# A new order around the first scores, in the short units and in the last units of a cross-attention and expert kernel

## The chip, the cores and the metric

One core of a Trainium2 chip runs the whole program. The metric is the device time of one execution in microseconds (us), as the median of several runs. PE is the matrix engine (TensorE), ACT is ScalarE, DVE is VectorE, POOL is GpSimd, and SP is the engine whose queue issues most of the DMAs.

## The reference

`x` is 32 x 100 x 512 and the context 32 x 722 x 512, all in float32. With 16 heads of 32:

```python
x = x + xattn(layernorm(x), ctx, ctx, WQ, WK, WV, Wfc, bfc)
x = x + ffn(layernorm(x), gate_w, Wg, Wu, Wd, Ws_g, Ws_u, Ws_d)

def xattn(Q, K, V, ...):
    q, k, v = heads(Q @ WQ.T), heads(K @ WK.T), heads(V @ WV.T)
    scores = q @ k.T / sqrt(32)
    scores = where(tril(ones(Sq, Skv)), scores, -inf)
    return softmax(scores) @ v ... @ Wfc.T + bfc

def ffn(h, ...):
    probs = softmax(h @ gate_w.T).transpose(0, 2, 1)       # 16 experts
    w, idx = top_k(probs, 12)                              # 12 tokens per expert and batch row
    out = scatter_add(((gelu(xt @ Wg.T) * (xt @ Wu.T)) @ Wd.T) * w)
    return out + (gelu(h @ Ws_g.T) * (h @ Ws_u.T)) @ Ws_d.T   # one shared expert
```

The mask is causal and a row of `x` has 100 positions, so only the first 100 positions of the context count, and the kernel takes only those: 3200 tokens on both sides.

## The kernel before

Products that feed the result are computed from a high and a low half of each operand in three matmuls (`mm3`): the high half is a cast to a shorter matmul format on ACT, the low half is the rest, formed by a subtraction on DVE or POOL. In the text "split" is this pair of steps.

**Stages.** The prologue loads and splits the weights of K, V and Q and computes keys and values of context blocks 0 and 1 (256 tokens each). Then come 32 attention units, `u = 0` to `31`. Unit `u` stands for a superblock of four batch rows (`sb = u // 4`, 400 tokens) and a group of four heads (`c = u % 4`, 128 columns). Units 0 to 28 run in one loop, and units 29 to 31 (`NU - 3` to `NU - 1`) and what is left behind them are written out one after the other in `last_units`. Behind the attention follow the shared expert and the 16 experts (`F.run`), which the diff does not touch.

**What one unit of the loop does**, in the order of the code:
- SP issues the loads: `kload(u)` (keys back from DRAM, `kt`), `ctx_load`, `x_load` and `xt_load` (rows and columns of x).
- `scores(u - 1)`: 16 small matmuls into the one set of score banks (`sc`), from `q` and `kt`.
- `y_keep(u - 3)` splits the output of `values` (ACT, then DVE) and so frees its bank.
- `sm_max(u - 1, 0 / 1)`: eight masked maxima each on DVE; `sm_sub`: the subtraction on POOL.
- `xt_split` splits 128 columns of x of the next superblock; `qproj(u)`, and `qkeep(u)` copies the result to `q` on ACT.
- `sm_exp(u - 1, 0 / 1)` on ACT, `sm_sum` (sum and reciprocal) on DVE, `sm_mul` on POOL.
- `p_turn(u - 2, 0..3)` transposes the probabilities on PE into the two `ms` banks, and `p_keep` copies them to `pt` on ACT.
- `kproj` and `vproj` compute a chunk of keys and a block of values of a coming context block; `kkeep` and `vkeep` copy them out of their bank on ACT and write them to DRAM (`kD`, `vD`). There are two banks `kv`, shared with `qproj`.
- `ctx_split(jn, d)`: cast on ACT, low half on POOL. `x_stats` (DVE) and `x_rstd` (POOL) give the scale of each row, which `sm_exp` applies; the mean is taken out of the weights of Q instead, by `wq_sum` (DVE), `wq_mean` (PE) and `wq_keep` (DVE, then a split).
- `values(u - 2)` multiplies the copies `pt` with `v` (loaded by `vload`, 800 KB for four units).

A context block from 2 on has three groups of 128 tokens but four chunks of keys, so in every fourth unit (u = 4, 8, ..., 28) there is a `kproj` and no `vproj`. These are the short units: their `values` come right behind the last two transposes.

**The order.** PE, ACT, DVE, SP and, in the attention, POOL run their instructions in the order in which the code issues them. An instruction that waits holds up all that stands behind it on its engine, and a DMA waits in SP's queue in the same way. Tiles come from rings of a fixed number of buffers (two `ms` and two `kv` banks, one `sc`, two `kt`, three `xr`, four `cr`, five `p`), and a new tile waits for the last reader of the buffer that it takes.

**The last units.** `pr` prepares the first 384 tokens of the expert part while units 29 to 31 run: `load_x`, `bias` (POOL), `fc` (PE), `add` (DVE), `stats` (DVE), `rsqrt` (POOL), `norm` (DVE), `store` (a write to DRAM), `turn` (transposes on PE, cast on ACT, low half on DVE), each for the tiles 0, 1, 2 of 128 tokens. `F.preps[1]` does the same for the next 256 tokens. `F.chunk_load`, `chunk_cast` (ACT) and `chunk_low` (POOL) bring and split the first expert weights, and `F.begin` starts the first `gu` matmuls.

Lines of the profile: L56 all `mm3` matmuls, L104 and L105 the cast and the low half of `split`, L138 and L139 the same of `ctx_split`, L223 `kkeep`, L229 `kload`, L234 `vload`, L249 `qkeep`, L259 `scores`, L270 `sm_max`, L279 `sm_sub`, L285 `sm_exp`, L290 and L291 `sm_sum`, L296 `sm_mul`, L302 `p_turn`, L307 `p_keep`, L317 `values`, L1059 `bias`, L1068 `add`, L1082 `rsqrt`, L1089 `norm`, L1000 and L1001 `turn`.

Of the kernel before, what the change touches and what calls it, by code (L numbers as in the profile page):

```python
# [7 lines left out]
F32 = mybir.dt.float32  # L8
# [52 lines left out]
def attention(tc, K, F):  # L61
    nc = tc.nc
    with ExitStack() as ctx, ExitStack() as kvctx:
# [153 lines left out]
        def kkeep(j, c, pk):  # L217
            t0, n = KSTART[j] * 128, KVB[j] * 128
            if j < 2 and c > 1:
                kk = qp.tile([128, SB], F32, name="q")  # L220
            else:
                kk = kkp.tile([128, KMAX], F32, name="kk")
            nc.scalar.copy(kk[:, 0:n], pk[:, 0:n])  # L223
            nc.sync.dma_start(K.kD[:, c, t0:t0 + n], kk[:, 0:n])
# [107 lines left out]
        def prologue():  # L332
# [48 lines left out]
            for c in range(NC4):  # L381
                kkeep(1, c, kproj(1, c))
                if c == 0:
                    wq_sum(0, wq[0])
                    wq_sum(1, wq[1])
                    kload(0)
                    for b in range(4):
                        x_load(0, b)
                else:
                    ctx_split(2, c - 1)  # L390
                if c == 1:
                    wq_mean(0)
                    wq_keep(0, wq[0])
                    xt_split(0, 2)
                if c == 2:
                    xt_split(0, 3)
                    wq_mean(1)
                    wq_keep(1, wq[1])
                if c > 1:
                    wq_sum(c, wq[c])  # L400
            xt_load(1, 0)
            ctx_load(3, 0)
            vkeep(1, 0, vproj(1, 0))
            return wq
# [16 lines left out]
        def last_units(pr):  # L421

            gp, mt = nc.gpsimd, pr.pt

            def maxes(u):
                for hb in range(2):
                    sm_max(u, hb)
                    sm_sub(u, hb)
# [3 lines left out]
            kload(u)  # L432
            for i in range(pr.nt):
                pr.load_x(i)
            y_keep(u - 3)
            kload(u + 1)
            vload(nsb - 1)
# [19 lines left out]
            pr.bias(0)  # L457
            maxes(u - 1)
            pr.bias(1)
# [3 lines left out]
            turns(u - 2, 0, 1)  # L463
            sm_exp(u - 1, 0)
            keeps(u - 2, 0, 1)
            sm_exp(u - 1, 1)
            pr.fc(1)
            for hb in range(2):
                sm_sum(u - 1, hb)
                sm_mul(u - 1, hb)  # L470
            turns(u - 2, 2, 3)
            keeps(u - 2, 2, 3)
            pr.norm(0)
            pr.add(1)
            kload(u + 1)
            F.chunk_load()
            values(u - 2)
# [4 lines left out]
            pr.store(0)  # L482
            pr.bias(2)
            pr.stats(1)
            pr.rsqrt(1)
            maxes(u - 1)
            pr.norm(1)
            qkeep(u, qproj(u))
# [4 lines left out]
            keeps(u - 2, 0, 1)  # L493
            sm_exp(u - 1, 0)
            sm_exp(u - 1, 1)
            pr.fc(2)
            sm_sum(u - 1, 0)
            sm_mul(u - 1, 0)
            pr.store(1)
            turns(u - 2, 2, 3)  # L500
            keeps(u - 2, 2, 3)
            sm_sum(u - 1, 1)
            sm_mul(u - 1, 1)
            pr.pt = lambda: ps_kv.tile([128, D], F32, name="kv").rearrange("p (c t) -> p c t", c=NC4)
# [3 lines left out]
            pr.add(2)  # L508
            pr.turn(1)
            pr.stats(2)  # L510
            F.chunk_cast(0, 0)
            pr.rsqrt(2)
# [11 lines left out]
            pr.norm(2)  # L524
# [11 lines left out]
            pr.store(2)  # L536
# [22 lines left out]
        with tc.manual_schedule(engines={mybir.EngineType.Pool}):  # L559
            wq = prologue()  # L560
            for u in range(NU - 3):
# [40 lines left out]
                if u == 0:  # L602
                    for b in range(3):
                        x_stats(0, b)
                    wq_mean(2)
# [10 lines left out]
                x_stats(*xn)  # L616
                if xn[1] == 3:
                    x_rstd(xn[0])
                if a is not None:
                    sm_exp(a, 1)  # L620
                    sm_sum(a, 0)
                    sm_mul(a, 0)
# [3 lines left out]
                if c == 1:  # L626
                    vload(sb)
                if back is not None:
# [3 lines left out]
                    p_keep(back, 3)  # L632
                if kv and not vv:
                    kkeep(j, ck, pk)
                if a is not None:
                    sm_sum(a, 1)
                    sm_mul(a, 1)
                if jn in blocks:
                    ctx_split(jn, d)
                if u in FC_AT:  # L640
                    F.fc_split(FC_AT.index(u), fr)
                if u == 0:
                    wq_keep(2, wq[2], nc.gpsimd)
                    vkeep(1, 1, vproj(1, 1))
                if vv:
                    vkeep(j, ck, vproj(j, ck))
                if back is not None:
                    values(back)
# [713 lines left out]
```

## Time and profile before

| what | value |
|---|---|
| median of 3 runs | 1670.34 us (1667.94 to 1670.6) |
| the profiled execution | 1668.51 us |
| its span, from the first to the last instruction | 1666.7 us, mean granted PE clock 0.999 |
| PE busy (matmuls) | 1641.7 us, 98% |
| DVE, ACT, POOL busy | 916.7, 695.9, 627.6 us |
| attention (prologue and units) | to about 371 us of the span |
| one full unit, one short unit | about 10.4 us, about 8.6 us |

Times in the text count from the start of the span. In a line of the timeline the columns are: start, duration, engine, line, operation, output and inputs with their shapes, and in brackets how long the engine had stood idle just before and what released it. In a line of the waits: who waited for whom, the total in us, how many times, the longest. In a line of the windows: the stretch and its length, then for each engine the busy us and the number of instructions, then the granted PE clock, the share of the DMA engines and the GB/s.

### The profile page before, as it was taken

To read this page: it belongs to the slowest core of one execution; us is meant where nothing else is said; L and a number is where in the kernel's file an instruction comes from. 1 tells how busy PE (TensorE), PEld (TensorE's weight loads), DVE (VectorE), ACT (ScalarE), POOL (GpSimd) and SP (SyncE) were. 2 spreads that over 40 slices of the span, in tenths; PEclk is the share of its full clock that TensorE was granted. 3 is DMA by queue.
4 is the path that set the end of the run, shared out by engine and by line. 5 is a ranking of instruction groups with operands and counts; after the bars stand their busy time and mean duration, and the time that the engine had idled before them with its cause. 6 is when DMAs were issued, how large, how long until landed. Compare 5 with 4: busy or idle time off the path is not lost.

```text
span 1666.7 us, 27942 instructions
## 1 busy us (share of the span) xinstructions
PE 1641.7 (98%) x10722; PEld 1503.5 (90%) x10722; DVE 916.7 (55%) x2175; ACT 695.9 (42%) x1152; POOL 627.6 (38%) x502
## 2 busy tenths in 40 slices
PE   8999999999999999999999999999999999999999
PEld 7788888879989998999999999999999999999998
DVE  5778777665433434343665555555555555555542
ACT  4666666553111111112444444444444444444442
POOL 1878777680110011010653344443344343344001
PEclk9999999999999999999999999999999999999999
DMA  7566655565312223211455555455555455555452
GB/s 236 167 188 204 196 176 169 194 192 187 114 62 84 76 90 126 82 46 41 155 172 161 161 167 154 153 150 161 163 160 161 153 149 163 163 155 163 138 160 61
DMA packets 113637, 244.02 MB, mean 146 GB/s; under 512 B 16625, under 2 KB 64978, under 8 KB 113504
## 3 DMA queue, kind: packets, MB, share of 16 engines
q1 hardware_dynamic: 100000, 216.54, 39.7%
q0 software_dynamic: 13088, 25.22, 7.9%
q8 instruction: 84, 1.38, 0.3%
q10 hardware_dynamic: 416, 0.48, 0.1%
q14 instruction: 49, 0.40, 0.1%
HBM read 188.46 MB, written 53.73 MB: 145 GB/s over the span
## 4 chain that ended last, share of the span: by engine, by line
PE 91%; DVE 2%; ACT 2%; POOL 2%; DMA 1%; issue 1%; SPq 0%; ACTq 0%; POOLq 0%; DVEq 0%
PE gu L56 49%; PE dn L56 24%; PE kv L56 9%; PE m L56 3%; PE ms L302 2%; PE ms L317 2%; POOL p L279 1%; PE sc L259 1%; DVE p L270 1%; ACT p L285 1%; ACT pt L307 1%; DMA xr<-xT 1%; DVE y L105 0%; DMA raw<-wA 0%; PE m L1143 0%
## 5 line engine op out<-in xcount | busy, mean ns | idle before, releaser
L56 PE MATMUL gu<-xh,whl 128*128 128x384 f32 (+1 forms) x3200 | 641.3, 332 | 0.0
L56 PEld LDWEIGHTS gu<-xh,whl 128*128 128x128 f32 x3200 | 555.8, 188 | 20.3 <-issue 1.3
L967 POOL DMA_INDIRECT gx<-xnD,iq x192 | 245.4, 1278 | 395.4 <-DVE big L1010 296.3
L56 PE MATMUL dn<-whl,hh 128*128 128x512 f32 x1168 | 366.3, 395 | 0.0
L770 DVE TENSOR_TENSOR whl<-wraw,whl 128x1536 fp32r<-128x1536 f32 x142 | 249.7, 1759 | 197.7 <-ACT whl L769 197.7
L56 PE MATMUL gu<-xl,whl 128*128 128x384 f32 (+1 forms) x1600 | 335.8, 331 | 0.0
L56 PEld LDWEIGHTS gu<-xl,whl 128*128 128x128 f32 x1600 | 279.1, 188 | 0.0
L804 ACT CAST hh<-g 128x384 fp32r<-128x384 f32 (+1 forms) x200 | 101.0, 505 | 407.6 <-DVE g L801 407.6
L56 PEld LDWEIGHTS dn<-whl,hh 128*128 128x128 f32 x1168 | 215.7, 188 | 35.7
L801 DVE TENSOR_TENSOR g<-g,gu 128x384 f32<-128x384 f32 (+1 forms) x200 | 108.2, 541 | 253.6 <-PE gu L56 247.3
L769 ACT CAST whl<-wraw 128x1536 fp32r<-128x1536 f32 x142 | 209.8, 1477 | 56.1 <-PE dn L56 53.1
L56 PE MATMUL dn<-whl,hl 128*128 128x512 f32 x584 | 230.5, 395 | 0.0
L800 ACT ACTIVATE g<-gu 128x384 f32<-128x384 f32 (+1 forms) x200 | 96.2, 481 | 232.6 <-PE gu L56 232.5
L805 DVE TENSOR_TENSOR hl<-g,hh 128x384 fp32r<-128x384 f32 (+1 forms) x200 | 111.6, 558 | 114.2 <-ACT hh L804 114.2
L1022 POOL DMA_INDIRECT out_dram<-x,isl x48 | 77.7, 1619 | 171.0 <-ACT x L1021 161.3
L56 PEld LDWEIGHTS dn<-whl,hl 128*128 128x128 f32 x584 | 109.6, 188 | 26.0
L279 POOL TENSOR_TENSOR p<-p,mx 100x800 f32<-100x800 f32 x64 | 105.7, 1672 | 43.0 <-DVE mx L270 42.4
L296 POOL TENSOR_TENSOR p<-p,sm 100x800 f32<-100x800 f32 x64 | 97.2, 1524 | 29.1 <-DVE sm L291 27.8
L270 DVE CUSTOM_DVE_ANT_0 p<-sc,mask 100x100 f32<-100x100 f32 x512 | 95.3, 256 | 0.0
L1059 POOL TENSOR_TENSOR x<-x,bfc 128x512 f32<-128x512 f32 x23 | 30.6, 1354 | 154.7 <-DMA x<-x 154.7
L285 ACT ACTIVATE p<-p,rstd 100x400 f32<-100x400 f32 x128 | 73.7, 624 | 20.3 <-POOL p L279 20.3
L1011 ACT CAST xh<-big 128x512 fp32r<-128x512 f32 x59 | 36.6, 621 | 101.1 <-DVE big L1010 101.1
(158 smaller groups left out, 1579.3 us busy)
## 6 DMA issues: line engine op xcount, KB each, us to landing
wraw<-wE SPq DMA_DIRECT2D x144, 768.0 KB
yD<-y SPq DMA_DIRECT2D x31, 400.0 KB
xr<-xT SPq DMA_DIRECT2D x32, 200.0 KB
vD<-vt SPq DMA_DIRECT2D x25, 256.0 KB
kt<-kD SPq DMA_DIRECT2D x32, 200.0 KB
v<-vD SPq DMA_DIRECT2D x8, 800.0 KB
xnD<-xn SPq DMA_DIRECT2D x25, 256.0 KB
out_dram<-x SPq DMA_DIRECT2D x25, 256.0 KB
```

Of the source, the lines that this page charges most:

```text
L56: r = nc.tensor.matmul(out, t[0][a], t[1][b], start=(first and i == 0), stop=(last and i == n - 1))
L270: nc.vector.tensor_tensor_reduce(out=p[:, bb, h, :], in0=sc[:, h, cs], in1=mask, scale=ISCALE, scalar=NEG, op0=ALU.add, op1=ALU.max, accum ...
L279: nc.gpsimd.tensor_tensor(pv, pv, mx[:, :, None].to_broadcast([S, 8, S]), ALU.subtract)
L285: nc.scalar.activation(p[:, bb], p[:, bb], AF.Exp, scale=rstd[:, b:b + 1])
L296: nc.gpsimd.tensor_tensor(pv, pv, sm[:, :, None].to_broadcast([S, 8, S]), ALU.mult)
L769: nc.scalar.copy(h, r)
L770: nc.vector.tensor_tensor(l, r, f32(h), ALU.subtract)
L800: nc.scalar.activation(g[:, 0:t], pg[:, 0:t], AF.Gelu)
L801: nc.vector.tensor_tensor(g[:, 0:t], g[:, 0:t], pu[:, 0:t], ALU.mult)
L804: nc.scalar.copy(hh[:, 0:t], g[:, 0:t])
L805: nc.vector.tensor_tensor(hl[:, 0:t], g[:, 0:t], f32(hh[:, 0:t]), ALU.subtract)
L967: nc.gpsimd.indirect_dma_start(out=g[:, k, :], out_offset=None, in_=self.K.xn.rearrange("t (a f) -> (t a) f", f=128), in_offset=bass.Indir ...
```

## The change

The diff touches only the order of the attention, and one copy is new.
- **First keys.** `kkeep` copies the first 400 tokens of key chunk 0 from the banks straight into `kt` on DVE, in two pieces (256 and 144 columns), and `kload(0)` goes.
- **Centring and splits.** `ctx_split(2, 0..2)` move to the end of the prologue. `wq_keep(2)` and `wq_keep(3)` move from units 0 and 1 to the middle and end of unit 1, behind exponentials of the first softmax; `xt_split(1, 0)` moves from unit 0 to the end of unit 1 and `xt_split(1, 1)` to unit 2, where `xt_split(1, 2)` is as well. Unit 1 has an order of its own. `x_load` and `x_stats` run one unit further ahead.
- **Short units.** They have no `ctx_split`; the unit before does two. The two context loads that belong to them are likewise issued together. In six of them (u = 4 to 24) `scores(u)` stand ahead of `values(u - 2)`, where the flag `ahead` tells the next unit to leave its own scores out and to put `y_keep` behind the first maxima.
- **Last units.** `vload` of the last superblock comes ahead of the x rows, and `bias`, `fc`, `add`, `stats`, `rsqrt`, `norm`, `store`, `qproj` and the transposes of units 30 and 31 stand in a new order.

```diff
@@ kkeep
             nc.scalar.copy(kk[:, 0:n], pk[:, 0:n])
+            if c == 0 and j < 2:
+                if j == 0:
+                    cur["k", 0] = ktp.tile([128, SB], F32, name="kt")
+                m = min(n, SB - t0)
+                nc.vector.tensor_copy(cur["k", 0][:, t0:t0 + m], pk[:, 0:m])
             nc.sync.dma_start(K.kD[:, c, t0:t0 + n], kk[:, 0:n])
@@ prologue
                     wq_sum(0, wq[0])
                     wq_sum(1, wq[1])
-                    kload(0)
                     for b in range(4):
                         x_load(0, b)
-                else:
-                    ctx_split(2, c - 1)
+                if c == 3:
+                    ctx_split(2, 0)
...
             xt_load(1, 0)
+            x_load(1, 0)
             ctx_load(3, 0)
             vkeep(1, 0, vproj(1, 0))
+            ctx_split(2, 1)
+            ctx_split(2, 2)
@@ last_units
             u = NU - 3
             scores(u - 1)
             kload(u)
+            vload(nsb - 1)
             for i in range(pr.nt):
                 pr.load_x(i)
             y_keep(u - 3)
             kload(u + 1)
-            vload(nsb - 1)
...
             pr.bias(0)
+            pr.bias(1)
             maxes(u - 1)
-            pr.bias(1)
             pr.stats(0)
             pr.rsqrt(0)
             qkeep(u, qproj(u))
             turns(u - 2, 0, 1)
+            keeps(u - 2, 0, 1)
             sm_exp(u - 1, 0)
-            keeps(u - 2, 0, 1)
             sm_exp(u - 1, 1)
             pr.fc(1)
+            pr.norm(0)
             for hb in range(2):
                 sm_sum(u - 1, hb)
                 sm_mul(u - 1, hb)
             turns(u - 2, 2, 3)
             keeps(u - 2, 2, 3)
-            pr.norm(0)
             pr.add(1)
             kload(u + 1)
             F.chunk_load()
+            pr.store(0)
+            pr.bias(2)
             values(u - 2)
 
             u = NU - 1
             scores(u - 1)
             y_keep(u - 3)
-            pr.store(0)
-            pr.bias(2)
+            maxes(u - 1)
+            pr.fc(2)
+            pr.add(2)
             pr.stats(1)
             pr.rsqrt(1)
-            maxes(u - 1)
             pr.norm(1)
-            qkeep(u, qproj(u))
+            pr.stats(2)
+            pr.rsqrt(2)
             F.ask(1, lambda: ps_kv.tile([128, D], F32, name="kv"))
             F.preps[1].load_x(0)
             F.preps[1].load_x(1)
             turns(u - 2, 0, 1)
             keeps(u - 2, 0, 1)
+            qkeep(u, qproj(u))
+            turns(u - 2, 2, 3)
+            keeps(u - 2, 2, 3)
             sm_exp(u - 1, 0)
             sm_exp(u - 1, 1)
-            pr.fc(2)
-            sm_sum(u - 1, 0)
-            sm_mul(u - 1, 0)
+            pr.norm(2)
             pr.store(1)
-            turns(u - 2, 2, 3)
-            keeps(u - 2, 2, 3)
-            sm_sum(u - 1, 1)
-            sm_mul(u - 1, 1)
+            pr.store(2)
+            for hb in range(2):
+                sm_sum(u - 1, hb)
+                sm_mul(u - 1, hb)
...
             pr.turn(0)
             pr.pt = mt
             values(u - 2)
-            pr.add(2)
             pr.turn(1)
-            pr.stats(2)
             F.chunk_cast(0, 0)
-            pr.rsqrt(2)
...
-            pr.norm(2)
...
-            pr.store(2)
@@ the loop over units 0 to 28
-                xn = divmod(u + 3, NC4)
+                xn = divmod(u + 4, NC4) if u + 4 < NU else None
+                nov = kv and not vv
...
-                if jl in blocks and (jl, dl) != (3, 0):
-                    ctx_load(jl, dl)
-                if u + 4 < NU:
-                    x_load(*divmod(u + 4, NC4))
+                for dd in {3: (), 2: (2, 3)}.get(dl, (dl,)):
+                    if jl in blocks and (jl, dd) != (3, 0):
+                        ctx_load(jl, dd)
+                if u + 5 < NU:
+                    x_load(*divmod(u + 5, NC4))
...
-                if a is not None:
+                if a is not None and not ahead:
                     scores(a)
-                if u - 3 >= 0:
+                if u - 3 >= 0 and not ahead:
                     y_keep(u - 3)
                 if a is not None:
                     sm_max(a, 0)
                     sm_sub(a, 0)
+                    if ahead:
+                        y_keep(u - 3)
                     sm_max(a, 1)
                     sm_sub(a, 1)
-                if xs:
+                if u == 2:
+                    xt_split(1, 1)
+                if xs and u > 1:
                     xt_split(sb + 1, c)
                 qkeep(u, qproj(u))
+                if u == 1:
+                    vload(0)
...
                 if u == 1:
-                    wq_keep(3, wq[3])
-                if a is not None:
+                    sm_exp(a, 0)
+                    wq_keep(2, wq[2])
+                    sm_sum(a, 0)
+                    sm_mul(a, 0)
+                if a is not None and u > 2:
                     sm_exp(a, 0)
...
+                if u == 2:
+                    sm_exp(a, 0)
...
+                if u == 1:
+                    sm_exp(a, 1)
+                    sm_sum(a, 1)
+                    sm_mul(a, 1)
...
+                if u == 1:
+                    vkeep(j, ck, vproj(j, ck))
+                    wq_keep(3, wq[3])
+                    xt_split(1, 0)
...
-                if jn in blocks:
-                    ctx_split(jn, d)
+                for dd in {3: (), 2: (2, 3)}.get(d, (d,)) if u else (3,):
+                    if jn in blocks:
+                        ctx_split(jn, dd)
...
-                    wq_keep(2, wq[2], nc.gpsimd)
                     vkeep(1, 1, vproj(1, 1))
-                if vv:
+                if vv and u > 1:
                     vkeep(j, ck, vproj(j, ck))
+                ahead = nov and u < NU - 4
+                if ahead:
+                    scores(u)
                 if back is not None:
                     values(back)
```

More of the change, by code (lines that the diff above doesn't have):

```diff
@@ L423, in last_units, with kt_bank @@
             gp, mt = nc.gpsimd, pr.pt
+            def kt_bank():
+                return ps_kv.tile([128, D], F32, name="kv").rearrange("p (c t) -> p c t", c=NC4)
             def maxes(u):
@@ L493, in last_units @@
             keeps(u - 2, 0, 1)
+            qkeep(u, qproj(u))
+            turns(u - 2, 2, 3)
+            keeps(u - 2, 2, 3)
             sm_exp(u - 1, 0)
             sm_exp(u - 1, 1)
-            pr.fc(2)
-            sm_sum(u - 1, 0)
-            sm_mul(u - 1, 0)
+            pr.norm(2)
             pr.store(1)
-            turns(u - 2, 2, 3)
-            keeps(u - 2, 2, 3)
-            sm_sum(u - 1, 1)
-            sm_mul(u - 1, 1)
-            pr.pt = lambda: ps_kv.tile([128, D], F32, name="kv").rearrange("p (c t) -> p c t", c=NC4)
+            pr.store(2)
+            for hb in range(2):
+                sm_sum(u - 1, hb)
+                sm_mul(u - 1, hb)
+            pr.pt = kt_bank
             pr.turn(0)
@@ L560, in attention @@
             wq = prologue()
+            ahead = False
             for u in range(NU - 3):
@@ L596, in attention @@
                     sm_sub(a, 0)
+                    if ahead:
+                        y_keep(u - 3)
                     sm_max(a, 1)
                     sm_sub(a, 1)
-                if xs:
+                if u == 2:
+                    xt_split(1, 1)
+                if xs and u > 1:
                     xt_split(sb + 1, c)
                 qkeep(u, qproj(u))
+                if u == 1:
+                    vload(0)
                 if u == 0:
-                    for b in range(3):
+                    for b in range(4):
                         x_stats(0, b)
+                    x_rstd(0)
                     wq_mean(2)
@@ L615, in attention @@
                     p_keep(back, 1)
[L616 to L619, printed above, removed]
+                if u == 2:
+                    sm_exp(a, 0)
+                if xn:
+                    x_stats(*xn)
+                    if xn[1] == 3:
+                        x_rstd(xn[0])
+                if a is not None and u > 1:
                     sm_exp(a, 1)
@@ L625, in attention @@
                     kkeep(j, ck, pk)
-                if c == 1:
+                if u == 1:
+                    sm_exp(a, 1)
+                    sm_sum(a, 1)
+                    sm_mul(a, 1)
+                if c == 1 and u > 1:
                     vload(sb)
@@ L632, in attention @@
                     p_keep(back, 3)
+                if u == 1:
+                    vkeep(j, ck, vproj(j, ck))
+                    wq_keep(3, wq[3])
+                    xt_split(1, 0)
                 if kv and not vv:
                     kkeep(j, ck, pk)
-                if a is not None:
+                if a is not None and u > 1:
                     sm_sum(a, 1)
                     sm_mul(a, 1)
-                if jn in blocks:
-                    ctx_split(jn, d)
+                for dd in {3: (), 2: (2, 3)}.get(d, (d,)) if u else (3,):
+                    if jn in blocks:
+                        ctx_split(jn, dd)
                 if u in FC_AT:
```

## The prediction

> **What bounds the kernel now.** The page first: the matmuls of TensorE (PE) fill 98% of the span, so only PE's idle time and its slow stretches can be won.
>
> ```profile
> span 1666.7 us, 27942 instructions
> ...
> PE 1641.7 (98%) x10722; PEld 1503.5 (90%) x10722; DVE 916.7 (55%) x2175; ACT 695.9 (42%) x1152; POOL 627.6 (38%) x502
> ...
> PEclk9999999999999999999999999999999999999999
> ```
>
> Idle are 25.0 us. Next PE's timeline, where a bracket ends a line in which PE stood still and names its releaser. Everything that the diff touches runs before 376 us; from 400 to 700 us PE is busy 100%, so behind the attention nothing changes and any time won there reaches the end. From 25 to 371 us the brackets add to 18.4 us:
>
> ```profile
> 38.09 0.96 PE L259 MATMUL sc<-kt,q 32*100 32x100 f32 x32 [2.81 <-ACT q L249]
> ...
> 39.88 1.53 PE L56 MATMUL kv<-xnl,wh 128*128 128x400 f32 x4
> ...
> 50.55 0.99 PE L56 MATMUL kv<-xnh,wh 128*128 128x400 f32 x4 [1.33 <-ACT kk L223]
> ...
> 57.31 0.86 PE L302 MATMUL ms<-ident,p 100*100 100x100 f32 x8 [1.50 <-ACT pt L307]
> ```
>
> ```profile
> 200.05 0.89 PE L317 MATMUL ms<-pt,v 100*32 100x100 f32 x32 [0.86 <-ACT pt L307]
> 208.02 0.94 PE L302 MATMUL ms<-ident,p 100*100 100x100 f32 x8 [0.98 <-ACT pt L307]
> 241.20 0.89 PE L317 MATMUL ms<-pt,v 100*32 100x100 f32 x32 [0.86 <-ACT pt L307]
> ```
>
> The 0.86 comes seven times, 40 us apart (79.88 to 321.26): `values` of each short unit waits for ScalarE's copies of the probabilities. The last units hold 1.77, 1.27 and three small ones. Third, the clock behind the 2.81 (the second last number but one is PEclk):
>
> ```profile
> 40.00:41.00 1.00, 1.00 (x5) 0.99 (x4) 0.96 (x3) 0.00 (x0) 0.00 (x0) 0.50 0.00 0
> ```
>
> Last, the timeline of all engines and SP's waits for what holds those releasers:
>
> ```profile
> 37.12 0.53 ACT L104 CAST xnh<-xr 128x400 fp32r<-128x400 f32 x1 [6.75 <-DMA xr<-xT]
> ```
>
> ```profile
> SPq L229 <- DMA kD<-kk: 4.3, 1, 4.3
> ```
>
> ScalarE sat 6.75 us before a split of x whose DMA went out late, because SP stood 4.3 us on the key load; `qkeep(0)`, and so the first scores, were queued behind.
>
> **A: up to unit 3.** I lay the new order out with the durations of before (times are its clock). The two new DVE copies have no row: between 0.20 (128x48 copy from PSUM) and 0.56 (128x400 from PSUM, two inputs); I take 0.3 and 0.25. The first falls into DVE's 1.29 us idle before 11.35. The second waits for `kproj(1, 0)` (about 20.5); the two `wq_sum` behind it on DVE (1.03 each) start at 20.9, not 18.83, and `wq_mean(0)` holds PE 0.15. Should the copy have to stand behind ScalarE's (0.37) of the same bank, A loses 0.4 at most. [...]
>
> ScalarE no longer waits 1.54 for `cr` at 24.00, so the bank copies that held PE 0.47 and 0.71 come in time: that of `kkeep(1, 2)` ends at 25.2 (ScalarE then has one cast of wq and one of x before it, no more), that of `kkeep(1, 3)`, behind the second centring on DVE (26.3 to 27.0) and its cast, at 28.0. So `vproj(1, 0)` starts at 25.4 and `qproj(0)` at 28.35 (was 29.52). `qkeep(0)` follows it, and scores(0) follow `vproj(1, 1)` (2.93) at 34.0 instead of 38.09: the 2.81 is gone. Then the clock: it read 0.50 for 3.9 us behind that gap and twelve matmuls took 3.76 instead of 2.2; minus 1.55. [...] Unit 1: scores 0.89, `qproj` 2.24, `kproj` 2.24, `vproj` 2.93: scores(1) at 42.3 (was 48.26).
>
> Given back in unit 2: DVE carries in unit 1 sixteen maxima (2.94), two centrings (0.67 each) and low halves (0.69), two sums with reciprocals (1.2 each), `x_stats` (0.87), a split (0.6): it starts the next maxima at 46.8, 4 us late, since it must wait for POOL and ScalarE between. POOL's subtractions end at 49.9 and 51.6 (1.67 each behind a first maximum at 48.2), the second exponential at 52.8 (1.15), `kkeep(2, 1)` at 53.25, and copies 2 and 3 of the probabilities, queued behind it on ScalarE, at 54.1: `values(0)` starts at 53.75, 1.65 after `vproj`, and its transposes wait 0.4. Two splits of x there (0.6 to 1.8 each, 1.80 being a row beside POOL's subtraction) can add 0.5, unit 3 waits 0.7 to 1.1. scores(3) come at 65.75 to 66.6 against 72.10: A = minus 5.8, bounds 4 and 7. Moved DMAs: without `kload(0)` the four x rows go out at 23.7 instead of 28.7 and land by 30.3 at the 300 GB/s of that stretch, when `x_stats` needs them; `vload(0)` stands on SP for the last write of `vD`, ahead of the key write of unit 1, which nobody reads for three units; `xt_load(1, 3)` stands there until 46.8, needed at 56.
>
> **B: short units.** Six of seven (not u = 28) put 0.83 of scores between the transposes and `values`; ScalarE's copies need 0.86 from the last transposes on; should they be late by more (the exponential before them waits on POOL), the excess shows again as a wait of `values`. The inputs of scores are ready: the score banks were read 3 us earlier. The next unit's maxima then start at 242.1 instead of 243.3 (behind a sum that ends 242.08), and POOL, without the low half of context (1.0) and the rstd pair (1.27) there, starts subtracting 1.1 us earlier: the chain moves ahead as much as PE. Two context splits in the unit before fit: ScalarE had 0.81 idle before `vt`, POOL 1.95 before its subtraction, against 0.54 and 1.0 (unit 11, with a split of Wfc as well, may lose 0.2). `y_keep` of the next unit moves behind the first maxima: its bank is wanted by the second transposes at 244.4, and DVE is through with it at 244.1. `rstd` goes to the unit before, where POOL has room; the doubled context loads on SP meet free tiles, since their splits now come a unit earlier. The 0.98 at 208 (the split of the gate's weights, 1.45 on DVE ahead of the maxima) stays. B = 6 x 0.83 = minus 5.0; bounds minus 5.2 and minus 1 (wait back in the next unit).
>
> **C: last units.** v is issued 3.2 us earlier, so the 1.77 goes, but not all is won: ScalarE's copies ended only at 339.47. New on POOL: bias(1) (1.30) stands ahead of both subtractions; they end at 338.2 instead of 337.1, both exponentials now precede copies 2 and 3, `values(28)` starts at 339.95 (was 340.61). On DVE norm(0) now stands before the sums and waits for POOL's rsqrt until 339.25; the products end at 344.15 (were 342.2), bias(2) at 345.45, subtractions at 348.45, rsqrt(1) 349.4. Scores(31) start at 350.85 (were 352.27): minus 1.4. But DVE still owes norm(1), stats(2), a wait for rsqrt(2), norm(2) (352.7), two sums (2.4), two low halves (1.4) and y(29) (0.55): 357.05, before 354.98. The next transposes need y(29)'s bank: PE, done with `fc(0)` at 354.6, waits 2.45. Then transposes and keeps, `fc(1)` 358.75 to 361.65, and the exponentials push the last xh to 363.6: the expert part starts at 363.65, before 362.20. C = plus 1.4; bounds minus 2 and plus 3.5, as two POOL waits more or less decide.
>
> **Sum.** 5.8 + 5.0 - 1.4 = 9.4. The profiled execution took 1668.5 (span 1666.7), so 1659.1; the median of before is 1.8 above that execution and its runs spread 2.7, so I say 1660. Faster or slower by 0.2% (3.3 us) is about what can be told from no change.
>
> **Rivals.**
> - *C also wins.* If the norms find POOL free (0.58 against the 2.61 that norm(0) took beside POOL's products), DVE is through near 355: C = minus 2, 1657. Against: I count three waits there. 0.17.
> - *The clock halves again.* 2.45 us idle at 354.6 is close to the 2.81 that halved it for 3.9 us; 1.77 did not. Price 1.9: 1662. 0.12. [...]
> - *B moves its wait.* Transposes 3 of the following unit already start the moment their bank is copied (x8 took 0.95, not 0.86, at 248.06). If the chain does not come earlier, B keeps 1: 1664. 0.09.
> - *Slower.* x rows 0 and 1 (256 KB each) now queue behind v (800 KB), whose wait in before ended 13.3 us after its issue. At that pace v lands at 337.3, x0 at 341.6, x1 at 345.9. In unit 30 add(0) stands first on DVE, with y(27), the maxima and all else behind it; on POOL bias(1) stands ahead of both subtractions. bias(1) then ends at 347.2, the subtractions at 350.2, `values(28)` starts at 351.9: 11.9 late, plus 1.9 of clock, 4.4 slower than before: 1675. It decides from x1 at 333.9, one for one, and passes the time of before at 341.5. Against: those 13.3 us were shared with some 1.7 MB still queued ahead of v; at the 350 to 400 GB/s that the queues move from 324 to 333, the 3.1 MB up to x1 (yh, yl, kt, v, x0, x1, the first issued at 322.4) are through by 331 to 333. 0.07.
> - *The edit is void*: scores(u) not ahead because its bank is busy. The maxima before end 3 us earlier; with the last rival 0.01.
>
> The forecast has 0.54. The range 1655 to 1667.5 takes A from 4 to 7, C's bounds and B's rival; outside stay the slow case and sums of bad ends. Faster 0.84, same 0.08 (A and B both at their low ends, or B's rival with C at plus 3.5), slower 0.08.
>
> **What would show it.** Right: no 2.81 and no 0.50 clock near 35 us; scores(3) 5 to 6.5 us earlier; one 0.86 left of seven; the 1.77 gone; a new wait of 2 to 2.5 before transposes of unit 30, released by DVE's y; `gu` starting 8 to 11 earlier than 362.20. Wrong: 0.8 waits on `pt` in the units behind the short ones; DVE standing on x in unit 30; `gu` at 359 or later.

## The result, and the profile after

| | median | range | runs |
|---|---|---|---|
| before | 1670.34 us | 1667.94 to 1671.87 | 5 |
| after | 1660.53 us | 1659.32 to 1664.56 | 5 |

The ratio is 0.9951, with a 95% interval of 0.9933 to 0.9968. The forecast was 1660. The profiled execution of after is the longest of its five, 1664.56 us (span 1662.8), and its mean granted clock the lowest, 0.996; three of the others had 0.999 and took 1659.3 to 1660.5. In the new kernel `scores` are L264, `p_turn` L307, `p_keep` L312, `values` L322, `kload` L234, `vload` L239, `load_x` L1092, `bias` L1095, `add` L1104. The page of after:

```profile
span 1662.8 us, 27950 instructions
...
PE 1645.8 (99%) x10722; PEld 1509.3 (91%) x10722; DVE 911.2 (55%) x2178; ACT 697.2 (42%) x1152; POOL 623.9 (38%) x501
```

PE's matmuls take 4.1 us longer than before while its idle time falls from 25.0 to 17.0: part of the time is lost in slow matmuls, not in waits. PE's timeline (start, duration, what, and in brackets the idle time just before and its releaser):

```profile
22.82 0.49 PE L184 MATMUL ms<-pt,avg 128*128 128x128 f32 x2 [0.39 <-DVE pt L180]
...
34.45 0.96 PE L264 MATMUL sc<-kt,q 32*100 32x100 f32 x32
...
55.23 1.56 PE L322 MATMUL ms<-pt,v 100*32 100x100 f32 x32 [2.97 <-ACT pt L312]
...
154.90 0.86 PE L307 MATMUL ms<-ident,p 100*100 100x100 f32 x8 [0.69 <-ACT pt L312]
...
312.65 0.89 PE L322 MATMUL ms<-pt,v 100*32 100x100 f32 x32 [0.86 <-ACT pt L312]
...
329.72 0.91 PE L307 MATMUL ms<-ident,p 100*100 100x100 f32 x4 [3.53 <-DVE y L105]
...
351.97 0.94 PE L307 MATMUL ms<-ident,p 100*100 100x100 f32 x8 [1.10 <-DVE xl L1037]
...
358.71 0.97 PE L56 MATMUL gu<-xh,whl 128*128 128x384 f32 x4 [0.50 <-ACT xh L1036]
```

The 2.81 before the first scores, the 1.77 of the last units and the 0.98 at 208 are gone; one 0.86 of seven is left (at 312). New are 2.97 before `values(0)`, 3.53 between the first two transposes in unit 30, and some small ones. At both large waits the clock halves, the second time 1.5 us before PE resumes. Windows of after (the third number from the end is the granted PE clock):

```profile
57.00:58.00 1.00, 1.00 (x29) 1.00 (x28) 0.57 (x1) 0.77 (x2) 1.00 (x2) 0.50 0.62 242
...
330.00:331.00 1.00, 1.00 (x6) 0.90 (x5) 1.00 (x13) 0.28 (x1) 1.00 (x2) 0.50 0.77 308
```

It stays at 0.50 from about 55 to 61.9 and from 328.2 to 335. Starts of stages, in us from the start of the span:

| | scores(0) | scores(1) | scores(3) | scores(27) | scores(28) | first `gu` | span |
|---|---|---|---|---|---|---|---|
| before | 38.09 | 48.26 | 72.10 | 313.47 | 322.08 | 362.20 | 1666.7 |
| after | 34.45 | 42.60 | 69.45 | 304.86 | 313.48 | 358.71 | 1662.8 |

So in this execution A (to unit 3) gave 2.65, B (to scores(27)) 5.95, C took 5.1 back (45.23 from scores(28) to `gu`, 40.12 before), and from `gu` to the end it is 1304.1 against 1304.5. A won less and C lost more than predicted; two rows show what stands behind C. SP's and DVE's timelines of after:

```profile
315.43 0.66 SPq L239 DMA_DIRECT2D v<-vD  x1
316.18 1.49 SPq L1092 DMA_DIRECT2D x<-x  x3
```

```profile
328.49 0.69 DVE L1104 TENSOR_TENSOR x<-kv,x 128x512 f32<-128x512 f32 x1 [6.15 <-DMA x<-x]
```

v (800 KB) goes out ahead of the x rows, row 0 lands 12 us after its issue, and `add(0)` holds DVE for 6.15 us. `y_keep` is queued behind it; its output is the releaser of PE's 3.53.

### The profile page after: what moved, and what is told of

Read it like the earlier page. It is cut to its first block, busy times and chain, and to the rows that moved or that the text cites. A ratio compares the mean times of both kernels' runs of the same rounds, so it can differ in the third digit from the quotient of the medians.

```text
span 1662.8 us, 27950 instructions
## 1 busy us (share of the span) xinstructions
PE 1645.8 (99%) x10722; PEld 1509.3 (91%) x10722; DVE 911.2 (55%) x2178; ACT 697.2 (42%) x1152; POOL 623.9 (38%) x501
## 4 chain that ended last, share of the span: by engine, by line
PE 92%; DVE 2%; POOL 2%; DMA 1%; ACT 1%; issue 1%; SPq 0%; POOLq 0%; ACTq 0%; DVEq 0%
PE gu L56 49%; PE dn L56 24%; PE kv L56 10%; PE m L56 3%; PE ms L307 2%; PE ms L322 1%; PE sc L264 1%; POOL p L284 1%; DMA x<-x 1%; DMA raw<-wA 1%; DVE p L275 0%; ACT p L290 0%; POOL p L301 0%; PE m L1179 0%; DVE pt L180 0%
## 5 line engine op out<-in xcount | busy, mean ns | idle before, releaser
L284 POOL TENSOR_TENSOR p<-p,mx 100x800 f32<-100x800 f32 x64 | 104.3, 1646 | 39.8 <-DVE mx L275 39.7
L1095 POOL TENSOR_TENSOR x<-x,bfc 128x512 f32<-128x512 f32 x23 | 30.6, 1352 | 160.2 <-DMA x<-x 154.1
```

Of the source, the lines that this page charges most:

```text
L284: nc.gpsimd.tensor_tensor(pv, pv, mx[:, :, None].to_broadcast([S, 8, S]), ALU.subtract)
```

## The experiments

The first eight start from after, and all but runs 3 and 8 change one thing. Times are medians; a ratio is to before, with its 95% interval.

**1. The x rows ahead of v again.**

```diff
-            vload(nsb - 1)
             for i in range(pr.nt):
                 pr.load_x(i)
+            vload(nsb - 1)
```

> The changed kernel, but in unit 29 the three x rows are issued ahead of v (v stays ahead of the write of y and of the key load). Theory (order in the queue): x0 landed 12.2 us after its issue only because v's 800 KB were ahead of it; now add(0) does not wait, the wait of 3.53 us before the second transposes of unit 28 is gone, and the half clock behind it too; values(28) may wait for v up to 0.5. Median 1656 to 1658, profile: no wait over 1 us between 322 and 345. Rival (the queues are simply full with 3 MB, whatever the order): x0 still lands after 327, the wait stays at 2 to 3.5 us and the time at 1659 to 1664.

1657.54 us (1656.73 to 1658.5), ratio 0.9929 [0.9916, 0.9943]: 3.0 below after. PE's timeline:

```profile
54.96 1.56 PE L322 MATMUL ms<-pt,v 100*32 100x100 f32 x32 [2.40 <-ACT pt L312]
...
330.27 0.89 PE L322 MATMUL ms<-pt,v 100*32 100x100 f32 x32 [0.75 <-ACT pt L312]
```

The 3.53 and its half clock are gone, v comes in time where it now stands, and `gu` starts at 352.66, 40.03 after scores(28), against 45.23. The order in SP's queue is the whole loss of C against before. (In the medians the step is smaller than the 6.1 us between the profiled executions, and the two intervals overlap.) The wait before `values(0)`, which this run leaves alone, is still there.

**2. The copies 2 and 3 of unit 0's probabilities earlier in unit 2.** `kproj` and these transposes and copies go ahead of the first exponential:

```diff
+                    p_late = kproj(j, ck)
+                    p_turn(back, 2)
+                    p_turn(back, 3)
+                    p_keep(back, 2)
+                    p_keep(back, 3)
                     sm_exp(a, 0)
+                    kkeep(j, ck, p_late)
```

> The changed kernel, but in unit 2 ScalarE copies the third and fourth transposes of unit 0 (and then the keys) ahead of the exponentials that they stood behind. Theory: values(0) waited 2.97 us only because these copies stood behind the second exponential, which waited for POOL; now values(0) follow vproj at once, and the half clock from 55 to 61 us goes in every execution. scores(2) at about 53.1 instead of 56.7; part of it (1 to 1.5) is given back before the first transposes of unit 3, whose products on POOL come no earlier. Gain 1.5 where the clock stayed full, 3.5 where it was halved: median 1657.5 to 1660, no execution above 1663. Rival (unit 2 and 3 are bound by DVE and POOL, the wait only moves): scores(3) at 69.4 less at most 0.5, median 1660 to 1661, and the wait of 2 to 3 us appears in unit 3.

1662.8 us (1659.79 to 1663.91), ratio 0.9959 [0.9945, 0.9972]. `values(0)` no longer waits, but unit 3 does:

```profile
56.53 0.89 PE L307 MATMUL ms<-ident,p 100*100 100x100 f32 x8 [0.73 <-POOL p L301]
62.12 0.86 PE L307 MATMUL ms<-ident,p 100*100 100x100 f32 x8 [2.58 <-ACT pt L312]
```

The copies were only the last link. What is late is unit 1's softmax, and PE meets it one unit later. The clock stays at 1.00 behind this 2.58. Scores(3) did come at 66.52, earlier than the rival had it, but the median did not fall and lies above both expectations; the trace does not say why.

**3. More work for PE where it waits.** The products of `vproj(2, 1)` and of `qproj` in unit 30 run twice, with the same result.

```diff
-            mm3(nc, ps, ...)
+            for _ in range(2 if (j, i) == (2, 1) else 1):
+                mm3(nc, ps, ...)
...
+            for _ in range(2 if u == NU - 2 else 1):
```

> The changed kernel with work added: the value projection of unit 2 and the query projection of unit 30 are computed twice into the same bank (24 matmuls more, about 5 us of PE), each just ahead of one of the two long waits (2.97 and 3.53 us). Theory (the waits halve the clock, in some executions, for about 3.5 us after the wait at a price of 2 each): the added matmuls fit into the waits, PE is never idle for over 1.5 us, the clock is 1.00 throughout in every execution and the time 1658 to 1660, at or below that of the changed kernel, though PE does more. Rival (the spread of the executions from 1659 to 1664.6 has another cause, the clock is only a sign): executions above 1662 come again, or the time is 2 to 5 us above that of the changed kernel because the added work is not hidden.

1661.86 us (1660.0 to 1663.25), ratio 0.9953 [0.9939, 0.9966], so 24 added matmuls cost nothing that can be told. PE's timeline:

```profile
55.62 0.89 PE L324 MATMUL ms<-pt,v 100*32 100x100 f32 x32 [0.28 <-ACT pt L314]
```

From the start of `values(0)` to scores(3) it took 12.12 us at a full clock, 14.22 in after: 2.1 is the price of that half clock (unit 3 alone took 11.29 and 12.73). The second doubling settles nothing: with it the wait of the last units moved (1.17 at 328.02 and 2.58 at 334.67), and the clock halved behind the 2.58. Two of the five executions took over 1662, the sign of the rival.

**4. `x_stats(1, 0)` from unit 0 into unit 1.**

```diff
+                if u == 1:
+                    x_stats(1, 0)
-                if xn:
+                if xn and u > 0:
                     x_stats(*xn)
```

> The changed kernel, but the statistics of the first x row of superblock 1 stand in unit 1, behind the first maxima, instead of in unit 0 ahead of them. Theory (DVE's wait of 1.32 us for that row at 35.3 pushes the whole softmax chain of units 0 and 1, and so the 2.97 us wait of values(0)): first maxima start 1.2 us earlier, values(0) waits 1.5 to 2.2, short enough for a full clock. Median 1657.5 to 1659.5. Rival (the chain is held elsewhere, by the splits of x beside POOL's subtractions in unit 2): values(0) still waits 2.6 to 3, time as that of the changed kernel, 1659 to 1664.

1664.2 us (1662.69 to 1664.65, 7 runs), ratio 0.9966 [0.9955, 0.9977]; `values(0)` waited 2.99, after's 2.97. The first maxima did start 1.0 earlier (35.23), but the 0.8 us of the statistics now stand behind them, and the maxima of unit 1 start at 48.12, after's 48.29. My theory of this run fell: that row of x is not what makes the maxima late. Why the median is 3.7 above after's, with overlapping intervals, stays open.

**5. Short units without scores ahead**, with their context splits still moved.

```diff
-                ahead = nov and u < NU - 4
+                ahead = False
```

> The changed kernel with the scores of the short units back behind values, at the start of the next unit; the context splits stay as changed. Theory (part B of the prediction: scores hide ScalarE's copies): six waits of 0.86 us before values come back, 5 us in all; units 4 to 28 take 5 us more and the median is 1664.5 to 1666.5 (the changed kernel had 1660.5). Rival (the context split and not the order of scores brought the gain, or the wait only moved): the waits before values are 0.4 or less without it, median 1660 to 1662.

1668.07 us (1666.11 to 1671.7, 11 runs), ratio 0.9992 [0.9983, 1.0001]. All six waits are back, one of them:

```profile
154.60 0.95 PE L322 MATMUL ms<-pt,v 100*32 100x100 f32 x32 [0.86 <-ACT pt L312]
```

Four units take 40.0 us again, 38.94 to 39.06 in after (but for one such group with new waits of 0.60 and 0.69): 1.0 for each of six, a little more than the wait itself. The 0.98 at 208 does not return, so the moved context splits removed that one. The median is 7.5 above after's, more than the 5 expected. The windows show a cost that neither the theory nor the rival had: behind two waits in a row (0.69 at 152.87, 0.86 at 154.60) the clock halves for 3.4 us, and unit 13 takes 11.8 us instead of 10.5:

```profile
156.00:157.00 1.00, 1.00 (x28) 0.91 (x24) 0.57 (x1) 0.52 (x2) 1.00 (x1) 0.50 0.82 220
```

**6. The last units of before**, everything else of after. The two lines stand for the whole function.

```diff
-        def last_units(pr):   # of after
+        def last_units(pr):   # of before
```

> The changed kernel with units 29 to 31 in the old order (v behind the x rows, biases, norms and fc where they were). Theory: the new last units lose (45.2 us from scores(28) to the first gu against 40.1 before, of which 3.5 are the wait for x0 and about 2 the half clock behind it, where it came); the old order gives the 40.1 again: median 1656 to 1658.5, as the kernel with the x rows ahead of v. Rival (as the prediction's first rival: the new order wins by itself, only x0 costs): the old order is 1 to 3 us slower than the kernel with the x rows ahead of v (1657.5): 1658.5 to 1660.5.

1657.81 us (1656.82 to 1662.9, 6 runs), ratio 0.9932 [0.992, 0.9944]. The old waits are back, and `gu` starts 41.6 after scores(28):

```profile
328.55 0.89 PE L322 MATMUL ms<-pt,v 100*32 100x100 f32 x32 [1.65 <-DMA v<-vD]
...
338.82 0.89 PE L322 MATMUL ms<-pt,v 100*32 100x100 f32 x32 [1.40 <-ACT pt L312]
```

So the new last units cost 2.7 us in the median (intervals overlap) and 3.6 by the trace, 45.23 against 41.6. The 41.6 holds a half clock of 3.4 us itself, behind the 1.40; before, with nearly the same waits and a full clock, took 40.12:

```profile
343.00:344.00 1.00, 1.00 (x4) 0.75 (x3) 1.00 (x12) 0.00 (x0) 1.00 (x2) 0.50 0.03 11
```

The rest of the change alone is 12.3 below before, 1670.09 in this comparison.

**7. First keys by DMA again**, as in before, everything else of after: the two copies of `kkeep` go, `kload(0)` returns.

```diff
-                nc.vector.tensor_copy(cur["k", 0][:, t0:t0 + m], pk[:, 0:m])
...
+                    kload(0)
                     for b in range(4):
                         x_load(0, b)
```

> The changed kernel with the first keys read back from DRAM: the two copies on DVE go, and the key load stands again on SP between the key write and the x rows. Theory (part A: SP stands 4 us for the key write and all loads behind it go out 4 to 5 us later): the statistics of the first x rows end near 39 instead of 34, the first maxima start 3 to 4 us later, values(0) waits 5 to 6.5 us instead of 2.97 and the clock halves every time; median 1664 to 1667. Rival (the loads behind it have slack, and the keys themselves land in time): scores(0) within 0.5 us of the changed kernel's 34.4, values(0) as before, median 1660 to 1662.

1666.83 us (1665.13 to 1669.63, 10 runs), ratio 0.9981 [0.9972, 0.999]: 6.3 above after. Scores(0) come at 33.22, even earlier; the time goes in what SP issues behind the key load. DVE waits 2.92 us for the first x rows, and the first maxima start at 39.81 instead of 36.20:

```profile
39.67 0.44 PE L56 MATMUL kv<-cxl,wh 128*128 128x384 f32 x1 [1.84 <-POOL cxl L139]
...
58.85 0.89 PE L317 MATMUL ms<-pt,v 100*32 100x100 f32 x32 [2.97 <-ACT pt L307]
```

`values(0)` waits as long as in after, not the 5 to 6.5 expected, because PE itself comes to it 3.6 us later.

**8. Several at once**: x rows first as in 1, `x_stats` as in 4, both centrings of wq (`wq_keep(2)`, `wq_keep(3)`) in unit 0, and scores ahead in unit 28 as well.

```diff
                     wq_mean(3)
+                    wq_keep(2, wq[2])
+                    wq_keep(3, wq[3])
...
-                ahead = nov and u < NU - 4
+                ahead = nov and u < NU - 3
```

> The changed kernel with the x rows ahead of v, the last two centrings of wq and their splits moved from unit 1 into unit 0 (right behind the statistics of the first rows), the statistics of the first row of superblock 1 behind the first maxima, and the scores of unit 28 ahead of its values too. Theory (DVE is what is late in units 1 and 2, and it idles in unit 0): the maxima of unit 1 start near 45 instead of 48.4, values(0) waits under 1 us, no half clock after 50 us, scores(3) at 64 to 66 instead of 69.4, one wait of 0.86 less: median 1652 to 1655. Rival (the wait only moves into units 1 to 3, as with the early copies): scores(3) at 68 or later, median 1656 to 1658.

1657.88 us (1655.19 to 1659.26), ratio 0.9922 [0.9909, 0.9935], no better than 1. Unit 28's 0.86 went, and 0.85 came at 317.81, where `fc(0)` waits for its y. Before `values(0)` the wait stayed:

```profile
55.20 1.56 PE L322 MATMUL ms<-pt,v 100*32 100x100 f32 x32 [2.76 <-ACT vt L203]
```

Of these 2.76, 1.8 pass until the copies end at 54.25, although the maxima of unit 1 start at 46.18 here. For the last 0.95 I take v's load, which had gone out 5 us later than in after; no run tried it alone.

**What holds `values(0)`.** The chain of unit 2 in after, from DVE's, POOL's and ACT's timelines:

```profile
46.03 1.00 DVE L105 TENSOR_TENSOR wl<-raw,wh 128x512 fp32r<-128x512 f32 x1 [0.69 <-ACT wh L104]
46.95 1.41 DVE L105 TENSOR_TENSOR xnl<-xr,xnh 128x400 fp32r<-128x400 f32 x1
48.29 0.25 DVE L275 CUSTOM_DVE_ANT_0 p<-sc,mask 100x100 f32<-100x100 f32 x1
```

```profile
49.90 3.34 POOL L284 TENSOR_TENSOR p<-p,mx 100x800 f32<-100x800 f32 x2 [1.97 <-DVE mx L275]
```

```profile
53.27 1.15 ACT L290 ACTIVATE p<-p,rstd 100x400 f32<-100x400 f32 x2 [0.67 <-POOL p L284]
54.33 0.46 ACT L223 COPY kk<-kv 128x384 f32<-128x384 f32 x1
54.68 0.88 ACT L312 COPY pt<-ms 100x400 f32<-100x400 f32 x2
```

DVE takes unit 1's maxima at 48.29, though their scores are done at 43.6: the low halves of wq(3) and of x (1, 0) stand ahead of them. POOL, done with its low half of context at 47.93, stands idle for 1.97 us until the first eight of them are there. The last four runs work on this order, on top of run 1.

**9. The split of x (1, 0) behind the maxima.**

```diff
@@ end of unit 1
-                    xt_split(1, 0)
@@ unit 2, behind sm_sub(a, 1)
                 if u == 2:
+                    xt_split(1, 0)
                     xt_split(1, 1)
@@ unit 2, behind sm_exp(a, 1)
+                if u == 2:
+                    xt_split(1, 2)
                     sm_sum(a, 0)
                     sm_mul(a, 0)
```

> Base: x rows ahead of v (the version of 1657.5 us). In it values(0) waits 2.40 us, and the chain behind that wait begins on DVE, which starts the maxima of unit 1 at 48.02, 3.5 us after their scores, because the low halves of wq(3) (0.69 idle and 1.00) and of x (1.41) stand ahead. Here the split of x (1, 0) goes behind those maxima and (1, 2) behind the second exponential. Theory (DVE's order holds it): maxima of unit 1 at 46.6, the wait before values(0) 0.9 to 1.3, no half clock there, unit 3 in 11.3 us instead of 12.8, scores(3) at 66.3 to 67.0 instead of 69.23; median 1655 (1654.3 to 1656). Rival 1 (the wait is moved, as when the copies came early): the wait before values(0) shrinks, but unit 3 waits 2 us or more and its clock halves; scores(3) at 68 or later, median 1657 to 1658. Rival 2 (v or POOL is late by itself): the wait stays 2 or more.

1656.96 us (1656.08 to 1657.81), ratio 0.9924 [0.9911, 0.9938]. This kernel and the next also leave out the sum and the product of the first half of each softmax from scores(2) to scores(27), so their times say little and only units 1 and 2 are read. The maxima start at 46.60 as expected, the wait shrinks, and scores(3) come at 66.73, but the clock still halves, for 3.4 us. PE's timeline and the windows:

```profile
53.96 0.89 PE L322 MATMUL ms<-pt,v 100*32 100x100 f32 x32 [1.55 <-ACT pt L312]
```

```profile
57.00:58.00 1.00, 1.00 (x5) 0.99 (x4) 1.00 (x13) 0.00 (x0) 1.00 (x1) 0.50 0.79 232
```

**10. The split of wq(3) behind them too**, with only its centring left ahead.

```diff
-            split_wc(2, c, r, eng)
+            if c != 3:
+                split_wc(2, c, r, eng)
...
                 if u == 2:
+                    split_wc(2, 3, wq[3])
                     xt_split(1, 2)
```

> As the run before, and the split of the centred wq(3) also goes behind the second exponential of unit 1 in unit 2; only its centring stays ahead of the maxima. Theory: maxima of unit 1 at 45.2 to 45.6; now POOL limits, whose product (to 46.2) and low half of context end at about 47.2, so the subtractions begin at 47.2 instead of 49.63; the wait before values(0) 0 to 0.5; scores(3) 65.8 to 66.5; median 1654.5 (1653.8 to 1655.6). Rival 1 (wait moved to unit 3, which now also carries the split of wq): scores(3) at 67.5 or later, median 1656.5 or more. Rival 2 (v late): PE still waits 1 us or more at values(0) with the copies already done.

1656.44 us (1654.92 to 1657.88), ratio 0.9923 [0.991, 0.9937]. The maxima start at 44.47 and `values(0)` waits 0.75 at a full clock. The theory of DVE's order holds, with POOL's product and low half of context setting the rest.

**11. The same with all of the work in.**

> Both moves behind the maxima of unit 1 (split of x (1, 0) and split of the centred wq(3); x rows ahead of v), with all of the work in. In the run with the sums and products of the first halves left out from unit 3 on, values(0) waited 0.75 and unit 3 1.43 at a full clock and scores(3) began at 65.70. Theory (DVE's order held the wait): here values(0) waits 0.7 to 0.9, unit 3 1.4 to 2, scores(3) 65.6 to 66.3, later units as in the version of 1657.5 us, so 3 us less: median 1655 (1654 to 1656.5). Rival (the wait is only passed on): with the sums in, unit 3 or 4 waits 2.5 or more with a half clock behind it; scores(4) gain less than 1 us; median 1657 to 1658.

1656.72 us (1655.28 to 1657.16), ratio 0.9926 [0.9912, 0.9939]. PE's timeline:

```profile
53.07 0.89 PE L323 MATMUL ms<-pt,v 100*32 100x100 f32 x32 [0.76 <-ACT pt L313]
61.50 0.86 PE L308 MATMUL ms<-ident,p 100*100 100x100 f32 x8 [1.44 <-ACT pt L313]
```

In the profiled executions the step is there in full: scores(3) at 65.89 against 69.23 in run 1, `gu` at 349.39 against 352.66, span 1653.5 against 1656.7. In the medians only 0.8 of these 3.3 can be seen, less than expected; four of the five clocks are 1.000, so slow matmuls are not what the other executions lost.

**12. In unit 2 also the sums ahead of the low half of x (1, 2)**, the first of them ahead of that of wq(3).

```diff
                     sm_exp(a, 1)
-                    if u == 2:
-                        split_wc(2, 3, wq[3])
-                        xt_split(1, 2)
                     sm_sum(a, 0)
                     sm_mul(a, 0)
+                    if u == 2:
+                        split_wc(2, 3, wq[3])
...
                     sm_sum(a, 1)
                     sm_mul(a, 1)
+                    if u == 2:
+                        xt_split(1, 2)
```

> As the run before, but in unit 2 DVE takes the sums of unit 1 ahead of the low half of x (1, 2), and the first of them ahead of that of wq(3). Theory (what is late in unit 3 is POOL's product, which waits for these sums): POOL's products start 1.5 earlier, the wait before the second transposes of unit 3 falls from 1.4 to 0.5 or less, scores(3) 64.7 to 65.3, median 1 us below the run before: 1654 (1653 to 1655.5). Rival (unit 3 waits for its own maxima, which start with their scores, and the exponentials behind them): the wait stays at 1 or more and the median is that of the run before.

1655.09 us (1654.71 to 1656.61), ratio 0.9918 [0.9904, 0.9931], the lowest median of all, 14.0 below before (1669.12 in this comparison); its interval lies below that of after and overlaps that of run 11. All five clocks are 1.000.

```profile
54.44 0.89 PE L323 MATMUL ms<-pt,v 100*32 100x100 f32 x32 [1.67 <-ACT pt L313]
62.21 0.86 PE L308 MATMUL ms<-ident,p 100*100 100x100 f32 x8 [0.80 <-ACT pt L313]
```

The second wait falls by 0.64, which was the point, though not to the 0.5 expected, and scores(3) come at 66.60, later than expected. The first wait is longer, although unit 1 is the same as in run 11. DVE's timeline of this run has the reason:

```profile
36.51 0.69 DVE L156 BATCH_NORM_STATS2 bst<-xt 100x6 f32<-100x512 f32 x1 [1.46 <-DMA xt<-x]
...
42.24 0.69 DVE L105 TENSOR_TENSOR wl<-raw,wh 128x512 fp32r<-128x512 f32 x1 [1.28 <-ACT wh L104]
```

In run 11 the same two stand at 34.47 (0.47 waited) and 40.45. The x rows of the first units land up to 2 us later in one execution than in another, and all of DVE's chain moves with them. Against this chain, 1.8 later here, the second transposes of unit 3 start only 0.7 later (62.21 against 61.50), so the move is worth about 1.1. That such landings are also what spread run 11's medians is likely, not shown.

## Why the prediction was right or wrong

The time was right, 1660.53 for 1660, and so was the direction; of the three terms only B was, in the profiled execution, about as large as worked out.

**A, minus 5.8 predicted, minus 2.65 in the profiled execution.** The first steps held: scores(0) at 34.45 (34.0), scores(1) at 42.60 (42.3), and no clock of 0.50 near 35. DVE's copy of 128x144 took 0.31 (0.25) and came behind ACT's copy of the same bank: it began at 21.49, ACT's had ended at 21.46, and the trace names that copy as the releaser of the 2.36 that DVE stood before it. PE waited 0.39 for it (at 22.82, for the `wq_sum` queued behind the copy on DVE), the 0.4 that I had allowed.

The step that failed is "it starts the next maxima at 46.8" in unit 2: it was 48.29, 1.5 late. I had priced the low half of x at 0.6 and the wait for ACT's cast of wq inside "between"; they measured 1.41 and 0.69, and the low half of wq 1.00 for 0.69. So the wait of `values(0)` was 2.97, not 1.65. Runs 9 to 11 show this, by taking these two out of the way: 2.40 became 1.55 and 0.76. `values(0)` began 1.5 late, and the clock, which the forecast had put into A's gain but not into its new wait, cost 2.1 more. The code up to unit 3 is the same in after and in runs 1, 5 and 6, and their scores(3) stand at 69.45, 69.23, 66.08 and 66.91. The two with a full clock there are at or near the 65.75 to 66.6 predicted.

When does it halve? Here idle times of 2.97, 2.76, 2.40, 1.55 and 1.40 us (after and runs 8, 1, 9 and 6) were followed by a clock of 0.50, and in run 5 two short ones of 0.69 and 0.86; 2.67 in run 6, 2.58 in run 2, 2.30 in run 5 and 1.67 in run 12 were not. It began between 1.5 us before PE resumed (after, at 328.2, in the wait of 3.53) and 1.9 us behind (run 6), and lasted 3.4 us (runs 5, 6, 9) or 6.8 (after, runs 1 and 8). In before the half clock behind the 2.81 lasted, by its windows, 3.4 us too (39.7 to 43.1), not the 3.9 that I had read. The windows of run 6, right behind its 2.67:

```profile
55.00:56.00 1.00, 1.00 (x48) 0.85 (x44) 1.00 (x2) 1.00 (x4) 0.66 (x1) 1.00 0.60 213
```

So the length of the gap alone does not decide here: in run 6 the 1.40 was followed by a half clock, the 2.67 was not. What does decide, no run shows. It is likely that the half clock also makes most of the spread of after's five executions, 5.2 us with mean clocks of 0.996 to 0.999; only one of them has a trace, and in run 4 an execution with 0.999 took 1664.25, as long as those with 0.996.

**B, minus 5.0 predicted, 5.95 measured.** Run 5 shows the mechanism and its size, 1.0 for each short unit. The 0.98 at 208 I had let stay; it went with the moved context splits. Unit 11, where I allowed 0.2, has a new wait of 0.60 (at 143.68), and the short unit 12 one of 0.69 (at 154.90). The rival "B moves its wait" did not come: the units right behind the short ones have no wait on `pt`.

**C, plus 1.4 predicted, plus 5.1 in the profiled execution, about plus 2.7 in the median (run 6).** The wait of 2 to 2.5 before the transposes of unit 30 did not come (1.10 and 0.31 stand there, behind the transposed rows of x). What came was the mechanism of the slower rival, the x rows queued behind v, at a smaller price. The step that failed is "through by 331 to 333", in the clock of before; in that of after, 8.6 us earlier at scores(28), it is 322.4 to 324.4, and x0 alone landed at about 328.4. The rival's point, x1 at 333.9, is 325.3 there, and x1 stands behind x0: passed by 3 us or more, and PE waited 3.53. I had the mechanism and its point; the windows of after show what was wrong in the rate (the last two numbers are the share of the DMA engines and GB/s):

```profile
316.00:320.00 4.00, 3.62 (x27) 3.14 (x26) 2.32 (x19) 3.14 (x8) 3.00 (x2) 1.00 1.06 386
320.00:324.00 4.00, 4.00 (x74) 2.95 (x73) 1.67 (x4) 1.50 (x3) 3.02 (x2) 1.00 1.07 252
324.00:328.40 4.40, 2.19 (x15) 1.93 (x13) 0.00 (x0) 0.89 (x2) 0.03 (x1) 0.97 0.98 309
```

The DMA engines are full throughout and move 3.9 MB at a mean of 315 GB/s until x0 is there, where I had 3.1 MB at 350 to 400. `gu` at 358.71 was, to 0.3 us, one of the signs that I had named for wrong; in run 1 it is at 352.66, inside the predicted 8 to 11 earlier. With the x rows first, C is minus 0.1 (40.03 against 40.12), both at a full clock, so the rest of the new order neither won nor lost.

**The sum.** 2.65 + 5.95 - 5.1 is 3.5 in the profiled execution, and 0.4 more behind `gu`, against 9.4 predicted. The median execution is 4 us better than the profiled one, with a mean clock of 0.999 against 0.996. In the profiled execution A and C were taken too favourably by 3.2 and 3.7 us and B too low by 1. The median execution lost less, very likely to the clock, and that brought the number back. No term of the forecast held this, so that the number came so close was luck. In the medians, the first keys are worth 6.3 (run 7), the scores ahead 7.5 (run 5) and the new last units minus 2.7 (run 6); taken out one at a time like this, they need not add up to the measured 9.8.

## What to carry to other kernels

When a stage is pulled forward, write down the landing time of every load that it reads before asking whether the engines keep up: here one swap of two lines in a queue was worth 3 us. A wait that ends in a copy on one engine may begin three engines earlier: here moving the last link only passed it on (2.58 in unit 3, run 2), while moving what stood ahead of the first link took it from 2.40 to 0.76 (runs 1 and 11). Idle times of PE between 1.40 and 2.97 us, and two shorter ones close together, were followed by slow matmuls in some places (at a price of 2.1 us behind the 2.97 of after) and not in others (2.67 in run 6): where such a wait is left, price it both ways, and read the granted clock of several executions.

## What the runs showed of the hardware

- An idle time of 1.40 us was followed by 3.4 us at a clock of 0.50 (run 6), and so were 0.69 and 0.86 with 0.9 between them (run 5); 2.67 in another place was not (run 6). 2.97 was followed by 6.8 us of it, at a price of 2.1 us up to scores(3) (after against run 3).
- Two low halves of x (128x400, both inputs in SBUF) took 2.47 us on DVE beside POOL's subtractions (at 51.20 in after), 3.01 in run 11 (at 47.55), and a single one 0.57 with POOL idle (at 52.46 in run 11).
- With v ahead in the queue, 256 KB of x took 12 us from issue (316.2 in after) to landing (about 328.4), with the DMA engines full (shares of 0.98 to 1.07) at 252 to 386 GB/s.
